# Four graph layers on one core: the row of attention scores goes to all partitions by two DMAs through a line in DRAM

## The chip, the cores and the metric

The kernel runs on one core of a Trainium2 chip. The core has a matrix engine (PE, with its weight loads shown as PEld), a vector engine (DVE), a scalar engine (ACT), a general engine (POOL, also called GpSimd) and a queue engine (SP) that issues DMAs. Each engine works through its own list of instructions in order and waits at a semaphore where the next one needs something that is not there yet. The metric is the device time of one execution in microseconds, as the median of several runs.

## The reference

The input is 128 graphs of 128 nodes with 256 features each, and one 128x128 adjacency matrix per graph. Four layers follow each other, each with a residual and a layer norm: first a gated graph network of three steps, then three graph attention layers.

```python
# layer 0: three steps of message passing with a GRU cell
for i in range(3):
    m = einsum('bnd,de->bne', h, weight[i])
    aggr = einsum('bst,bsd->btd', A, m)
    h = gru_cell(aggr, h, w_ih, w_hh, b_ih, b_hh)
x = layernorm(x + h)
# layers 1 to 3: attention
Wh = einsum('bnf,of->bno', x, W)
f_i, f_j = Wh @ a1, Wh @ a2
e = leaky_relu(f_i[:, :, None] + f_j[:, None, :], 0.2)
e = where(adj == 0, -inf_like, e)
x = layernorm(x + einsum('bij,bjo->bio', softmax(e, axis=2), Wh))
```

In the sum `f_i[:, :, None] + f_j[:, None, :]` the second term is the same row of 128 scores for every node i. That row is what this document is about: it is computed as a column (one score for each node, a node being a partition) and is needed as a row on all 128 partitions.

## The kernel before

The 128 graphs are worked on in 32 groups of G = 4. A group passes through `gru` (three steps) and then `gat` (three attention layers, `for l in range(3)`). All matrix products are in float32. The GRU products of a step are done by `strassen` (line 649, the great majority of the matmuls) into five PSUM buffers named gate; all other products and transposes use three PSUM buffers named bank. Work buffers of one size share a pool: `k2` has 27 buffers of 128x512 floats, `k4` has 18 of 128x1024, `v` has 36 of 128x4.

Nothing is issued in the order in which it is written. Every operation is handed to a `Plan` with the engines that may do it and a cost in ns for each. The plan walks through time: an operation starts when its inputs have come (the producer's end plus a latency for each pair of engines), when its engine is free, and when its buffers are; among those that are ready the more urgent goes first. It repeats the walk six times with due times taken from the walk before and keeps the shortest. Each engine's list is then written out in the order found. For a DMA the plan counts the issue on SP, then `LATENCY["SP"]` = 4000 ns, then a correction `lag`. `LATER` shifts the stages of a group against each other, so that GRU matmuls of one group stand between the attention steps of another.

In one attention layer of one group, in order: the column sums `f` (8 reductions on DVE, line 850, four for each side) and in layers 1 and 2 a scaling (line 854); the row; the sum with the mask and its maximum (line 885, DVE, four); the leaky ReLU (line 889, ACT); the exponential (line 906, ACT); a turn of the 128x128 blocks by `turned`, which splits the halves of the floats (line 404 or 406), issues a DMA transpose on SP (line 516) and joins the halves (line 510 or 406); in layers 1 and 2 a scaling (line 918); then on PE the product of attention and features (line 956), two evictions, the product with the weights (line 967), and the residual (line 973). The next layer's sums start from there.

The row itself is made, in the first 28 groups, by one PE transpose of `f` (line 862; `f` is a 128x128 buffer of its own pool with a score in every 32nd column, so that the rows of the four graphs fall on partitions 0, 32, 64 and 96), an eviction by ACT or DVE (line 866, shown as line 404 or 406 for the copy's helper), and four GpSimd partition broadcasts (line 869) into `e_`. That operation needs a GpSimd library, loaded at the start (line 997) and exchanged for the standard one after the last use. The last four groups (`LAST` = 4) make the row by four PE transposes (line 879) and read it from PSUM.

Two other places use SP: the loads of features and adjacency (lines 681, 682, 801) and the store of the result (line 982), and `thirds` (line 540), which turns the hidden state between GRU steps by three DMA transposes for the product with the adjacency matrix (line 716).

Of the kernel before, what the change touches and what calls it, by code (L numbers as in the profile page):

```python
# [10 lines left out]
F32 = mybir.dt.float32  # L11
# [5 lines left out]
P = 128  # L17
D = 256
KC = D // P
G = 4  # L20
GN = G * P
# [287 lines left out]
def adj_resnorm_kernel(  # L309
# [14 lines left out]
    nc = tc.nc  # L324
    B = x.shape[0]
    NG = B // G
    LAST = 4
# [2 lines left out]
    consts = ctx.enter_context(tc.tile_pool(name="consts", bufs=1))  # L330
    work = ctx.enter_context(tc.tile_pool(name="work", bufs=1))
    psum = ctx.enter_context(tc.tile_pool(name="psum", bufs=1, space=bass.MemoryType.PSUM))


    pools = {"gru": 4, "xs": 2, "am": 5, "k2": 27, "k4": 18, "f": 3, "mv": 4, "st": 6, "v": 36,
             "mb": 4, "gate": 5, "bank": 3}
    own = ({"k2": 7, "k4": 10, "gate": 0, "bank": 0, "v": 5, "st": 0}, {"k2": 3, "k4": 1, "bank": 0, "v": 4, "st": 0})
    floats = {"gru": 0, "k4": 1024, "xs": 1024, "f": 128, "mv": 8, "st": 6, "v": 4, "mb": GN // 2}
# [5 lines left out]
    slots = {t: [(psum if t in ("gate", "bank") else work).tile([P, w], F32, name=f"{t}{i}")  # L344
                 for i in range(n)] for t, (n, w) in tags.items() if w}

    def T(b):
        if b.at is None:
            width = 1
            for s in b.shape:  # L350
                width *= s
            at = slots[b.tag][b.slot][:, 0:width]
            if len(b.shape) == 2:
                at = at.rearrange("p (a b) -> p a b", b=b.shape[-1])
            elif len(b.shape) == 3:
                at = at.rearrange("p (a b c) -> p a b c", b=b.shape[-2], c=b.shape[-1])
            b.at = at
        return b.at

    def bank():  # L360
        return Buf("bank", GN)
# [3 lines left out]
        b.at = t  # L365
        return b

    for t in slots["f"]:
        nc.vector.memset(t, 0.0)

# [3 lines left out]
    ident = consts.tile([P, P], F32)  # L374
# [27 lines left out]
    def copy(e, dst, src):  # L402
        if e == "ACT":
            nc.scalar.copy(dst, src)  # L404
        else:
            nc.vector.tensor_copy(dst, src)  # L406
# [431 lines left out]
    def gat(g, xc, no, stage):  # L838
# [3 lines left out]
        for l in range(3):  # L842
            prio = stage(g, STEPS + l)
            if g == 0:
                score_weights(l, (prio[0], -2))
            f, fi = Buf("f", G, P // G), Buf("v", G)
            side = lambda h, f=f, fi=fi: T(f)[:, :, 0] if h else T(fi)
            for h in (1, 0):
                for b in range(G):
                    plan.op({"DVE": 345}, lambda e, b=b, h=h, l=l, side=side, xc=xc: nc.vector.scalar_tensor_tensor(  # L850
# [2 lines left out]
                if l:  # L853
                    plan.op({"DVE": 78}, lambda e, h=h, side=side, rstd=rstd: nc.vector.tensor_mul(
                        side(h), side(h), T(rstd)), reads=[((fi, f)[h], b) for b in range(G)] + [rstd],
                        writes=[((fi, f)[h], b) for b in range(G)], prio=prio, port=BOTH)
            e_, pT, y = Buf("k2", G, P), Buf("k2", G, P), Buf("k4", G, D)
            top, nmax, den, rden = Buf("v", G), Buf("v", G), Buf("v", G), Buf("v", G)
            b_ = bank()
            if g < NG - LAST:  # L860

                plan.op({"PE": 109}, lambda e, b_=b_, f=f: nc.tensor.transpose(
                    T(b_)[:, 0:P], T(f).rearrange("p b h -> p (b h)"), ident),
                    reads=[(f, b) for b in range(G)], writes=[b_], prio=prio)
                row = Buf("k2", P)
                plan.op({"ACT": 160, "DVE": 207}, lambda e, b_=b_, row=row: copy(e, T(row), T(b_)[:, 0:P]),
                        reads=[b_], writes=[row], prio=prio)
                for b in range(G):
                    plan.op({"POOL": 292}, lambda e, row=row, b=b, e_=e_: nc.gpsimd.partition_broadcast(  # L869
                        T(e_)[:, b, :], T(row)[b * P // G:b * P // G + 1, 0:P]), reads=[row], writes=[(e_, b)], prio=prio, port=BOTH, holds=False)  # L870
# [5 lines left out]
            else:  # L876
                def fn(e, b_=b_, f=f):
                    for b in range(G):
                        nc.tensor.transpose(T(b_)[:, b * P:(b + 1) * P],
                                            T(f)[:, b, 0:1].to_broadcast([P, P]), ident)  # L880
# [40 lines left out]
            else:  # L921
                b_ = bank()
# [119 lines left out]
```

## Time and profile before

| What | Value |
|---|---|
| median of 3 runs | 2499.49 us (2498.88 to 2499.88) |
| the profiled execution | 2499.94 us |
| its span, first to last instruction | 2497.9 us |
| mean granted PE clock | 0.997 |
| SP's DMA issues | 366 DMA transposes, 128 loads and stores of x, adj and out, 13 loads of weights |
| DMA queue of SP | 455952 packets, 158.65 MB, 29.9% of the 16 DMA engines' span |
| partition broadcasts (line 869) | 336, 138.4 us of POOL |
| transposes of line 862 | 84 |

The profile lists busy time for each engine, groups of instructions by line with their mean time, what each engine waited for, and for DMAs the time from the issue to the landing, that is until the semaphore has its full count. A matmul is pipelined: the time shown for one overlaps the next, so what it takes from PE is the distance from its start to the next start.

### The profile page before, as it was taken

The page shows a single profiled execution, that of the slowest core. Times are in us where ns is not written, and L with a number is a line of the kernel's source. Part 1 is how long each engine was busy: PE and PEld are TensorE (multiplying, and loading weights), DVE is VectorE, ACT ScalarE, POOL GpSimd, SP SyncE. Part 2 cuts the span into 40 slices and gives each one's busy share as a digit, 9 for nine tenths or more (in the row PEclk, how much of TensorE's full clock was granted, in tenths as well). Part 3 has the DMA queues.
Part 4 walks back from the last instruction along what each step waited for, and adds up shares of the span by engine and source line. Part 5 has one row for each costly group of instructions (what it writes and reads, how often), then busy time and mean ns, then how long its engine had stood idle before and what let it go on. Part 6 is the DMA issues. An engine that isn't in the chain of part 4 may idle for free.

```text
span 2497.9 us, 42545 instructions
## 1 busy us (share of the span) xinstructions
PE 2469.1 (99%) x13492; PEld 2180.1 (87%) x13492; DVE 2164.0 (87%) x6461; ACT 1925.7 (77%) x4835; POOL 781.9 (31%) x999
## 2 busy tenths in 40 slices
PE   8999999999999999999999999999999999999998
PEld 7888888888888888888888888888888888888877
DVE  6789888989888988889988889988889988877797
ACT  6578777888778787788887778887787888666577
POOL 2232233422334332334333334233333332211001
PEclk9999999999999999999999999999999999999999
DMA  5223233233333332333242233333233333110101
GB/s 148 56 56 64 60 76 69 64 81 60 76 64 73 72 81 60 73 68 73 68 77 68 61 80 68 73 71 74 60 77 68 76 65 68 26 39 18 38 1 35
DMA packets 456609, 161.38 MB, mean 65 GB/s; under 512 B 389184, under 2 KB 454720, under 8 KB 456384
## 3 DMA queue, kind: packets, MB, share of 16 engines
q1 hardware_dynamic: 455952, 158.65, 29.9%
q8 instruction: 106, 1.74, 0.3%
q14 instruction: 119, 0.97, 0.1%
q10 hardware_dynamic: 432, 0.01, 0.0%
HBM read 45.89 MB, written 16.78 MB: 25 GB/s over the span
## 4 chain that ended last, share of the span: by engine, by line
PE 86%; DVE 6%; ACT 4%; DMA 2%; issue 1%; POOL 0%; POOLq 0%; ACTq 0%; DVEq 0%
PE gate L649 63%; PE bank L967 10%; PE bank L956 6%; PE bank L716 3%; PE bank L719 2%; DVE nobody L850 2%; DMA k<-k 1%; DVE k L973 1%; ACT k L906 1%; ACT k L404 1%; DMA xs<-in_x_dram 1%; ACT k L510 1%; DVE k L406 1%; DVE k L654 1%; PE bank L822 0%
## 5 line engine op out<-in xcount | busy, mean ns | idle before, releaser
L649 PE MATMUL gate<-k,whs 128*128 128x256 f32 x4032 | 1205.2, 381 | 3.5 <-ACT k L742 1.6
L649 PE MATMUL gate<-k,wcs 128*128 128x256 f32 x4032 | 1199.3, 379 | 1.3 <-ACT wcs L404 1.3
L649 PEld LDWEIGHTS gate<-k,wcs 128*128 128x128 f32 x4032 | 766.0, 190 | 105.8 <-ACT wcs L404 1.8
L649 PEld LDWEIGHTS gate<-k,whs 128*128 128x128 f32 x4032 | 741.2, 190 | 107.8 <-ACT k L742 9.6
L654 DVE TENSOR_TENSOR k<-gate,k 128x512 f32<-128x512 f32 x576 | 388.4, 685 | 125.6 <-PE gate L649 80.4
L563 POOL TENSOR_TENSOR v<-v,neghalf 128x4 f32<-128x4 f32 x128 | 159.3, 1244 | 843.5 <-DVE v L601 460.9
L967 PE MATMUL bank<-gwT,k 128*128 128x256 f32 x1536 | 349.6, 380 | 1.6 <-DVE k L406 0.8
L967 PEld LDWEIGHTS bank<-gwT,k 128*128 128x128 f32 x1536 | 290.1, 190 | 43.7 <-DVE k L406 3.6
L850 DVE SCALAR_TENSOR_TENSOR nobody<-k,wa 128x256 bf16<-128x256 f32 x768 | 297.7, 427 | 0.7 <-ACT k L582 0.7
L753 ACT ACTIVATE k<-k,brz 128x256 f32<-128x256 f32 (+1 forms) x384 | 229.6, 624 | 71.1 <-DVE k L654 71.0
L618 POOL TENSOR_TENSOR k<-k,k 128x256 f32<-128x256 f32 x272 | 232.9, 867 | 104.1 <-DVE k L792 37.9
L404 ACT COPY k<-bank 128x512 f32<-128x512 f32 (+1 forms) x272 | 155.1, 572 | 112.0 <-PE bank L956 56.3
L735 ACT COPY k<-gate 128x512 f32<-128x512 f32 x288 | 167.9, 584 | 87.2 <-PE gate L649 83.7
L536 POOL TENSOR_TENSOR k<-k 128x512 f32<-128x512 f32 (+1 forms) x143 | 155.9, 1090 | 239.1 <-DVE k L792 189.4
L404 ACT COPY k<-k 128x512 bf16<-128x512 bf16 (+1 forms) x265 | 175.7, 694 | 53.8 <-DVE k L792 27.3
L869 POOL PARTITION_BROADCAST k<-k x336 | 138.4, 512 | 240.3 <-DVE k L406 149.1
L590 ACT ACTIVATE nobody<-k 128x256 bf16<-128x256 f32 x384 | 157.0, 415 | 60.5 <-DVE k L973 60.3
L510 ACT COPY k<-k 128x1024 uint16<-128x1024 uint16 x163 | 189.9, 1166 | 17.1 <-DMA k<-k 15.2
L956 PEld LDWEIGHTS bank<-k,k 128*128 128x128 f32 x1536 | 183.8, 192 | 11.0 <-DVE k L918 3.7
L956 PE MATMUL bank<-k,k 128*128 128x128 f32 x1536 | 190.2, 277 | 2.4 <-ACT k L510 1.5
L782 ACT ACTIVATE k<-k,bi 128x512 f32<-128x512 f32 x192 | 136.6, 726 | 66.4 <-DVE k L779 52.5
L973 DVE SCALAR_TENSOR_TENSOR k<-bank,v,k 128x256 f32<-128x256 f32 x384 | 166.9, 476 | 23.0 <-PE bank L967 22.8
(110 smaller groups left out, 3296.7 us busy)
## 6 DMA issues: line engine op xcount, KB each, us to landing
xs<-in_x_dram SPq DMA_DIRECT2D x32, 512.0 KB, 3.9
k<-in_x_dram SPq DMA_DIRECT2D x32, 512.0 KB, 4.1
out_dram<-k SPq DMA_DIRECT2D x32, 512.0 KB, 2.9
am<-in_adj_dram SPq DMA_DIRECT2D x32, 256.0 KB, 4.2
k<-k SPq DMA_TRANSPOSE x366, 3.1
k<-in_gnn_wT_dram SPq DMA_DIRECT2D x3, 256.0 KB, 4.7
k<-in_w_ihT_dram SPq DMA_DIRECT2D x2, 384.0 KB, 5.7
k<-in_w_hhT_dram SPq DMA_DIRECT2D x2, 384.0 KB, 6.7
```

The source lines that it names most:

```text
L404: nc.scalar.copy(dst, src)
L510: nc.scalar.copy(flat().bitcast(U16).rearrange("p (q h) -> p q h", h=2), T(rows).bitcast(U16).rearrange("p (h q) -> p q h", h=2))
L563: plan.op({"POOL": 980}, lambda e: nc.gpsimd.tensor_tensor(T(rstd), T(ve), neghalf, ALU.pow), reads=[ve], writes=[rstd], prio=prio, port=B ...
L618: nc.vector if e == "DVE" else nc.gpsimd).tensor_tensor(T(t)[:, j, :], a(), b(), ALU.subtract),
L649: nc.tensor.matmul(T(dst)[:, j * H:(j + 1) * H], T(w)[:, m, gt, :], moving(m, ms)[1](), start=first and n == 0, stop=n == len(todo) - 1, s ...
L654: plan.op({"DVE": 602}, lambda e: nc.vector.tensor_add(T(o)[:, :, j * H:(j + 1) * H], T(b_).rearrange("p (g n) -> p g n", g=2), T(part).re ...
L735: plan.op({"ACT": 475}, lambda e: nc.scalar.copy(T(dst), T(src)), reads=[src], writes=[(dst, 0), (dst, 1)], prio=prio)
L753: nc.scalar.activation(T(o)[:, gt, n0:n1], src(), AF.Tanh, bias=brz[:, gt * KC + c:gt * KC + c + 1], scale=0.5)
L850: plan.op({"DVE": 345}, lambda e, b=b, h=h, l=l, side=side, xc=xc: nc.vector.scalar_tensor_tensor(next(nobody[1]), T(xc)[:, b, :], 1.0, T( ...
L956: nc.tensor.matmul(T(b_)[:, b * P:(b + 1) * P], T(xc)[:, b, c * P:(c + 1) * P], T(pT)[:, b, :], start=True, stop=True)
L967: nc.tensor.matmul(T(b_)[:, (b - b0) * D:(b - b0 + 1) * D], T(aT[k])[:, b * P:(b + 1) * P], T(gwT)[:, l, k, :], start=(k == 0), stop=(k == ...
L973: nc.vector.scalar_tensor_tensor(T(y)[:, b, :], T(b_)[:, (b - b0) * D:(b - b0 + 1) * D], T(rden)[:, b:b + 1], T(xc)[:, b, :], op0=ALU.mult ...
```

## The change

In the first 28 groups the transpose, its eviction and the four broadcasts are replaced by two DMAs on SP. The first writes the 128x4 scores into a line of 512 floats in DRAM, in the order graph, node; the elements that follow each other in the line come from different partitions. The second reads that line once for each of the 128 partitions into `e_`. `f` becomes a 128x4 buffer of pool `v`; the pool `f` with its three memsets goes, and a pool `line` of four DRAM tiles comes. Both library loads go. The plan counts each DMA as 400 ns on SP with a lag of -1300 ns. The last four groups keep their way.

```diff
+    far = ctx.enter_context(tc.tile_pool(name="far", bufs=1, space=bass.MemoryType.DRAM))
-    pools = {"gru": 4, "xs": 2, "am": 5, "k2": 27, "k4": 18, "f": 3, "mv": 4, "st": 6, "v": 36,
+    pools = {"gru": 4, "xs": 2, "am": 5, "k2": 27, "k4": 18, "line": 4, "mv": 4, "st": 6, "v": 36,
...
-    for t in slots["f"]:
-        nc.vector.memset(t, 0.0)
...
+    ROW = -1300
...
-            f, fi = Buf("f", G, P // G), Buf("v", G)
-            side = lambda h, f=f, fi=fi: T(f)[:, :, 0] if h else T(fi)
+            f, fi = Buf("v", G), Buf("v", G)
+            side = lambda h, f=f, fi=fi: T(f) if h else T(fi)
...
-            b_ = bank()
             if g < NG - LAST:
-                plan.op({"PE": 109}, lambda e, b_=b_, f=f: nc.tensor.transpose(
-                    T(b_)[:, 0:P], T(f).rearrange("p b h -> p (b h)"), ident),
-                    reads=[(f, b) for b in range(G)], writes=[b_], prio=prio)
-                row = Buf("k2", P)
-                plan.op({"ACT": 160, "DVE": 207}, lambda e, b_=b_, row=row: copy(e, T(row), T(b_)[:, 0:P]),
-                        reads=[b_], writes=[row], prio=prio)
-                for b in range(G):
-                    plan.op({"POOL": 292}, lambda e, row=row, b=b, e_=e_: nc.gpsimd.partition_broadcast(
-                        T(e_)[:, b, :], T(row)[b * P // G:b * P // G + 1, 0:P]), reads=[row], writes=[(e_, b)], prio=prio, port=BOTH, holds=False)
-                if g == NG - LAST - 1 and l == 2:
-                    plan.op({"POOL": 7000}, lambda e: nc.gpsimd.load_library(library_config.standard),
-                            reads=[(e_, b) for b in range(G)], writes=[Buf(None)], prio=prio)
+                line = Buf("line", GN)
+                plan.op({"SP": 400}, lambda e, f=f, line=line: nc.sync.dma_start(
+                    T(line)[0].rearrange("(b q) -> q b", b=G), T(f)),
+                    reads=[(f, b) for b in range(G)], writes=[line], prio=prio, lag=ROW)
+                plan.op({"SP": 400}, lambda e, line=line, e_=e_: nc.sync.dma_start(
+                    T(e_).rearrange("p b q -> p (b q)"), T(line).to_broadcast([P, GN])),
+                    reads=[line], writes=[(e_, b) for b in range(G)], prio=prio, lag=ROW)
...
-        nc.gpsimd.load_library(library_config.all_libraries[10])
```

More of the change, by code (lines that the diff above doesn't have):

```diff
@@ L332, in adj_resnorm_kernel @@
     psum = ctx.enter_context(tc.tile_pool(name="psum", bufs=1, space=bass.MemoryType.PSUM))
-    pools = {"gru": 4, "xs": 2, "am": 5, "k2": 27, "k4": 18, "f": 3, "mv": 4, "st": 6, "v": 36,
+    far = ctx.enter_context(tc.tile_pool(name="far", bufs=1, space=bass.MemoryType.DRAM))
+    pools = {"gru": 4, "xs": 2, "am": 5, "k2": 27, "k4": 18, "line": 4, "mv": 4, "st": 6, "v": 36,
              "mb": 4, "gate": 5, "bank": 3}
     own = ({"k2": 7, "k4": 10, "gate": 0, "bank": 0, "v": 5, "st": 0}, {"k2": 3, "k4": 1, "bank": 0, "v": 4, "st": 0})
-    floats = {"gru": 0, "k4": 1024, "xs": 1024, "f": 128, "mv": 8, "st": 6, "v": 4, "mb": GN // 2}
+    floats = {"gru": 0, "k4": 1024, "xs": 1024, "mv": 8, "st": 6, "v": 4, "mb": GN // 2}
     tags = {t: (n, floats.get(t, 512)) for t, n in pools.items()}
@@ L343, in adj_resnorm_kernel @@
     plan = Plan({t: n for t, (n, _) in tags.items()}, own)
-    slots = {t: [(psum if t in ("gate", "bank") else work).tile([P, w], F32, name=f"{t}{i}")
+    spaces = {"gate": psum, "bank": psum, "line": far}
+    slots = {t: [spaces.get(t, work).tile([1 if t == "line" else P, w], F32, name=f"{t}{i}")
                  for i in range(n)] for t, (n, w) in tags.items() if w}
@@ L858, in gat @@
             top, nmax, den, rden = Buf("v", G), Buf("v", G), Buf("v", G), Buf("v", G)
-            b_ = bank()
             if g < NG - LAST:
-                plan.op({"PE": 109}, lambda e, b_=b_, f=f: nc.tensor.transpose(
-                    T(b_)[:, 0:P], T(f).rearrange("p b h -> p (b h)"), ident),
-                    reads=[(f, b) for b in range(G)], writes=[b_], prio=prio)
-                row = Buf("k2", P)
-                plan.op({"ACT": 160, "DVE": 207}, lambda e, b_=b_, row=row: copy(e, T(row), T(b_)[:, 0:P]),
-                        reads=[b_], writes=[row], prio=prio)
-                for b in range(G):
-                    plan.op({"POOL": 292}, lambda e, row=row, b=b, e_=e_: nc.gpsimd.partition_broadcast(
-                        T(e_)[:, b, :], T(row)[b * P // G:b * P // G + 1, 0:P]), reads=[row], writes=[(e_, b)], prio=prio, port=BOTH, holds=False)
-                if g == NG - LAST - 1 and l == 2:
-                    plan.op({"POOL": 7000}, lambda e: nc.gpsimd.load_library(library_config.standard),
-                            reads=[(e_, b) for b in range(G)], writes=[Buf(None)], prio=prio)
+                line = Buf("line", GN)
[5 more added lines that the diff above has]
+                    reads=[line], writes=[(e_, b) for b in range(G)], prio=prio, lag=ROW)
                 rows, keys, port = (lambda b, e_=e_: T(e_)[:, b, :]), lambda b: [], BOTH
             else:
+                b_ = bank()
                 def fn(e, b_=b_, f=f):
@@ L879, in fn @@
                         nc.tensor.transpose(T(b_)[:, b * P:(b + 1) * P],
-                                            T(f)[:, b, 0:1].to_broadcast([P, P]), ident)
+                                            T(f)[:, b:b + 1].to_broadcast([P, P]), ident)
                 plan.op({"PE": 437}, fn, reads=[(f, b) for b in range(G)], writes=[b_], prio=prio)
```

## The prediction

> **What bounds the kernel now.** First the page's busy times, then the same by stretches of the span (columns: stretch, length, then busy time and number of instructions of each engine, granted clock, DMA share, GB/s).
>
> ```profile
> PE 2469.1 (99%) x13492; PEld 2180.1 (87%) x13492; DVE 2164.0 (87%) x6461; ACT 1925.7 (77%) x4835; POOL 781.9 (31%) x999
> ```
>
> ```profile
> 0.00:100.00 100.00, 93.15 (x441) 77.39 (x442) 68.37 (x137) 60.35 (x116) 23.07 (x30) 1.00 0.40 106
> 100.00:600.00 500.00, 496.93 (x2723) 438.19 (x2722) 436.95 (x1234) 388.99 (x959) 164.57 (x209) 1.00 0.33 67
> 600.00:1100.00 500.00, 499.54 (x2771) 442.89 (x2770) 447.77 (x1353) 402.63 (x998) 180.00 (x230) 1.00 0.34 71
> ...
> 2400.00:2498.00 98.00, 81.62 (x484) 70.53 (x484) 81.87 (x432) 76.63 (x299) 13.97 (x13) 0.93 0.07 23
> ```
>
> PE never rests in the middle: it is idle 0.46 us of 500 from 600 to 1100, 3.07 us of 500 while the pipeline of groups fills, and 16.4 us of 98 at the end, when no GRU work is left to fill gaps. So the end is set by the amount of PE work and by what makes PE wait. A shorter or longer chain elsewhere counts only if PE's list, which is in order, meets it.
>
> The third view is PE's timeline around one row transpose (start, length, engine, line, operation, tiles), with the two steps that follow it on other engines; the fourth is PE's groups, each shape apart, for that line.
>
> ```profile
> 1066.82 0.59 PE L649 MATMUL gate<-k,wcs 128*128 128x256 f32 x2
> 1067.26 0.27 PE L862 MATMUL bank<-ident,f 128*128 128x128 f32 x1
> 1067.37 0.60 PE L649 MATMUL gate<-k,whs 128*128 128x256 f32 x2
> ...
> 1068.42 1.34 POOL L869 PARTITION_BROADCAST k<-k  x4 [5.97 <-DVE k L406]
> ...
> 1068.88 0.29 DVE L885 CUSTOM_DVE_ANT_0 k<-k,am 128x128 f32<-128x128 f32 x1
> ```
>
> ```profile
> L862 PE MATMUL bank<-ident,f 128*128 128x128 f32 x84 | 23.2, 276 | 0.4 <-DVE nobody L850 0.3
> ```
>
> The transpose delays the next matmul by 0.11 us (1067.26 to 1067.37), not by its 0.28 us. From its start to the first use of the row on DVE it is 1.6 us here, and 2.1 and 2.3 us for the other two layers of that period (1096.42 to 1098.47, 1128.53 to 1130.80): 2.0 us on the mean. DVE starts on the first of four broadcasts while POOL is still at the others.
>
> Last, the DMAs (tiles, issuing queue, count, size, median us from issue to landing) and who waited for landings (waiter, awaited, total us, times, longest).
>
> ```profile
> xs<-in_x_dram SPq DMA_DIRECT2D x32, 512.0 KB, 3.9
> out_dram<-k SPq DMA_DIRECT2D x32, 512.0 KB, 2.9
> k<-k SPq DMA_TRANSPOSE x366, 3.1
> k<-in_gat_w_dram SPq DMA_DIRECT2D x3, 256.0 KB, 4.5
> bi<-in_b_ih_dram ACTq DMA_DIRECT2D x1, 3.0 KB, 2.6
> ```
>
> ```profile
> ACT k L510 <- DMA k<-k: 15.2, 21, 2.1
> ...
> DVE k L406 <- DMA k<-k: 4.6, 5, 1.4
> ```
>
> Of 366 transposes 26 came too late for ACT or DVE, by 19.8 us together. PE felt little: its own waits name line 956 behind line 510 with 1.5 us and line 716 behind a landing with 0.3 us, 1.8 of 19.8 or 9%.
>
> **The change, part by part.** *Removed from PE:* 28 groups x 3 layers = 84 transposes at 0.11 us, 9.2 us, and the 0.4 us of idle time before them: -9.6 us. PE's built list has those 84 fewer and nothing else changed in number, so PE's work is 9.2 us less for certain. All else is about waits.
>
> *Removed from DVE, ACT and POOL:* 74 evictions on DVE at 0.284 us, 10 on ACT at 0.263 us, 336 broadcasts (138.4 us of POOL), three memsets, both library loads. The plan also shifts other work: by the built lists, 45 evictions of 0.684 us go from ACT to DVE, 24 half-splits from DVE (0.718) to ACT (1.05), 20 joins from ACT (1.166) to DVE (0.718), 17 scalings of line 918 (four instructions of 0.393 us each) to ACT. The sums nearly cancel: DVE about +11 us of 2164, ACT about -7 us of 1926. Both stay below PE, so I take 0; the cover is PE's own work, and without it the +11 us would be the price.
>
> *Added to SP:* 168 issues at 0.43 us (the weight loads' issue time) are 72 us. In the built list 51 of the 84 second DMAs stand right behind their own first, so SP waits there until the line has landed, some 2.2 us after a first issue of 0.43: at most 84 x 2.2 = 185 us. SP's transposes take 366 x 1.23 = 450 us of 2498, so the queue has room. Queued behind: in 46 of 84 cases the next entry is a transpose (line 516 or 540), and ACT or DVE waits for its landing, then PE. If all were ready and 2.2 us late, 101 us of lateness at 9% would be 9 us; if none was ready, 0. The other entries between are placed by what is ready when, so I take +1.
>
> *The row's way:* two landings in a row in place of 2.0 us. The trace has no scatter of 4-byte pieces to DRAM and no load that reads one line 128 times. For the first, the ends are 2.6 us (the 3 KB load `bi`) and 4.3 us (the 6 KB load `ga`, behind two others); the nearest by direction, the store of 512 KB, has 2.9. It has a 256th of that store's bytes, so I take 2.6. For the second, also 256 KB in 128 rows of 2 KB, the nearest is the load of `gat_w`, whose three landed in 3.4 to 5.0 us, the first with no sister ahead of it; the ends are 2.6 us (fastest load of `am`, 256 KB) and 4.5; I take 3.4. Sum 6.0 us (5.2 to 8.8), which is 4.0 us more than the 2.0 (3.2 to 6.8).
>
> What hides these 4.0 us is matmuls of other groups. I counted them in both built lists, between the last matmul of line 967 and the first of line 956 in the next layer of the same group, each at its start-to-start distance in the trace (0.22 us for 256 columns, 0.11 for 128). Over the first 2200 us there are 54 such gaps: mean 22.5 us before (17.9 to 25.6), 26.5 after (20.8 to 39.4). PE's list now leaves 3.9 us more. The need is 4.0, so I take 0, at the very edge. If the cover were gone, 84 x 4.0 = 336 us would be added.
>
> *The order itself:* before, the list repeats itself exactly from group to group (gaps 25.6 and 20.2); after, it never settles, and the gap between GRU steps 1 and 2 shrinks from 34 to 22 us (medians), though 18 us occurred before, in a stretch without a wait. The unsettled stretch of before, 100 to 600, has 3.07 us idle per 500 against 0.46: over the 1600 us that were regular, (3.07 - 0.46) x 3.2 = 8 us at most, nothing at least. Of its waits, line 956 behind line 510 (1.5 us) belongs to gaps shorter than any in the new list, so I take a quarter of the 8: +2. First load at the start (5.0 us wait) and last twelve layers at the end (same PE entries after the last GRU product): 0, as nothing in them changes.
>
> Sum: -9.2 - 0.4 + 1 + 2 = -6.6 us. The profiled execution took 2499.94 us, 2.0 of it outside its span of 2497.9, and lies 0.45 above the median of 2499.49. From 2499.94 it gives 2493.3, from the median 2492.9: 2493.
>
> [...]
>
> **The rivals.** *The gain is eaten by the order (same).* PE loses 9.2 us of work, but the unsettled list costs the full 8 us: 2499.5 - 9.6 + 8 + 1 = 2499. For it: the 3.07 us; against: no gap as short as the shortest before.
>
> *The row lands late (slower).* All 16 DMA engines read one 2 KB line, and DMA transposes are queued ahead. If the first takes 2.9 us and the second 4.0, as the 512 KB loads do, the row needs 4.9 us more where the list has 3.9: each is 1.0 us late. Then DVE stands at line 885, behind which the gate sums of line 654 are queued, for which PE waits, and line 956 comes late itself. 22 of the 54 gaps are under 25 us; scaled to 84 rows, 34 tight ones at 1.0 us make +34: 2499.5 - 9.6 + 34 = 2524. It decides from 0.3 us late (34 x 0.3 = 10), that is from 6.2 us for both landings. For it: my need is already at the edge. Against: 19.8 us of late transposes cost PE 1.8 us, and the first landing may be quicker than 2.6.
>
> **How the numbers follow.** Forecast, PE's work goes and the waits stay small: 0.43, own range 2488 to 2495. Eaten by the order: 0.17. Late row: 0.40, thereof some 0.12 above 2535. A change under 0.2% (5 us) can't be told from none here. So faster 0.43, same 0.17, slower 0.40. The range runs from 2487 (neither +1 nor +2, with 3 us of PE's other waits gone as three banks serve 84 fewer users) to 2535 (1.3 us late in the same 34); about 0.05 below, 0.12 above.
>
> **What would show it.** PE busy falls by 9 us and its count by 84; DVE's idle time at the reductions with the new mask line names the line's landing in under 20 us if I am right, in over 60 us if the row is late; the two DMAs' landings read 2.6 and 3.4; PE's idle time in 600 to 1600 stays under 3 us. Wrong would make it: landings above 6.2 us in sum, transposes landing at well over 3.1 behind the new waits on SP, or a last stretch with far more idle than 16.4 us.

## The result, and the profile after

The kernel with the two DMAs takes 3158.47 us (median of five runs, 3157.48 to 3159.13) where the kernel before takes 2499.49 us beside it (2498.27 to 2500.55). The ratio is 1.2637, 95% interval 1.2618 to 1.2655: slower by 26%, far outside the range, and the wrong way.

The page's first lines of the kernel after: its span, and each engine's busy time, share and number of instructions.

```profile
span 3157.2 us, 42018 instructions
...
PE 2624.7 (83%) x13408; PEld 2289.3 (73%) x13408; DVE 2171.5 (69%) x6430; ACT 1931.8 (61%) x4839; POOL 617.4 (20%) x648
```

DVE and ACT work as long as before, and PE has its 84 instructions fewer. PE's idle time grew from 28.8 us (2497.9 - 2469.1) to 532.5 us (3157.2 - 2624.7), and its busy time grew by 155.6 us although it has less to do. Together that is the 659.3 us by which the span grew. The next view, the kernel after in stretches (columns as in the same view of before), tells where, and why busy time grew.

```profile
0.00:100.00 100.00, 92.40 (x441) 76.89 (x442) 69.56 (x134) 60.79 (x117) 22.91 (x31) 1.00 0.42 106
100.00:600.00 500.00, 419.35 (x2180) 366.67 (x2179) 349.68 (x964) 306.23 (x729) 98.10 (x106) 0.92 0.30 60
600.00:1100.00 500.00, 413.19 (x2104) 359.87 (x2103) 341.96 (x1008) 311.68 (x780) 107.90 (x112) 0.91 0.33 62
...
2600.00:3157.00 557.00, 481.95 (x2490) 421.51 (x2488) 391.92 (x1320) 330.43 (x933) 74.15 (x77) 0.93 0.17 35
```

The first 100 us, before the first row is needed, are as before. From then on PE idles in every stretch for 13 to 20% of its time (86.8 us of 500 from 600 to 1100, against 0.46 before), and the granted clock is 0.90 to 0.93 instead of 1.00. The loss is spread evenly over the groups.

Now the DMAs of the kernel after (tiles, queue, count, size, median us from issue to landing), and below them the waits (waiter, awaited, total us, times, longest), DVE's and ACT's first, SP's own last.

```profile
out_dram<-k SPq DMA_DIRECT2D x32, 512.0 KB, 3.1
...
k<-line SPq DMA_DIRECT2D x84, 256.0 KB, 5.1
...
line<-v SPq DMA_DIRECT2D x84, 2.0 KB, 10.0
```

```profile
DVE k L880 <- DMA k<-line: 559.6, 76, 15.4
ACT k L884 <- DVE v L880: 518.8, 78, 16.1
PE gate L650 <- DVE k L655: 163.6, 26, 11.4
...
PE gate L650 <- ACT k L736: 129.9, 20, 14.7
PE gate L650 <- ACT k L743: 129.6, 24, 8.8
...
ACT k L511 <- DMA k<-k: 73.5, 26, 10.0
...
DVE k L406 <- DMA k<-k: 35.2, 11, 7.2
```

```profile
SPq L865 <- DMA line<-v: 724.2, 84, 13.3
```

The first DMA writes 2 KB and lands after 10.0 us (8.7 at the least, 14.3 at the most). The store of 512 KB to the same kind of memory still lands after 3.1. Two chains follow from it. DVE stands at the masked sum (line 880, 885 before) for 559.6 us, in 76 of 84 cases, and ACT behind DVE; PE then waits at line 650 for gate sums and evictions that are queued behind them (lines 655, 736, 743). SP, on the other side, stands at the second DMA in all 84 cases, 724.2 us in all, and DMA transposes behind it are issued late (lines 511 and 406: 108.7 us of waits against 19.8 before). The timeline of the kernel after around one row shows both (start, length, engine, line, operation; in brackets the idle time before it); the lines are SP's, DVE's and PE's.

```profile
1507.75 0.36 SPq L862 DMA_DIRECT2D line<-v  x1
1517.12 0.33 SPq L865 DMA_DIRECT2D k<-line  x1
1517.55 4.61 SPq L517 DMA_TRANSPOSE k<-k  x2
...
1522.30 0.29 DVE L880 CUSTOM_DVE_ANT_0 k<-k,am 128x128 f32<-128x128 f32 x1 [6.04 <-DMA k<-line]
...
1524.57 0.70 PE L650 MATMUL gate<-k,whs 128*128 128x256 f32 x2 [2.33 <-DVE k L655]
...
1530.75 1.22 PE L650 MATMUL gate<-k,whs 128*128 128x256 f32 x2 [4.18 <-ACT k L743]
```

Between the first issue (1507.75) and the second (1517.12) lie 9.4 us in which SP issues nothing, and two transposes go out right behind the second. The row is used at 1522.30, 14.6 us after the first issue, where the plan had counted twice 3.1 us.

### The profile page after: what moved, and what is told of

Read it like the earlier page. It is cut to its first block, busy times and chain, and to the rows that moved or that the text cites. A ratio compares the mean times of both kernels' runs of the same rounds, so it can differ in the third digit from the quotient of the medians.

```text
span 3157.2 us, 42018 instructions
## 1 busy us (share of the span) xinstructions
PE 2624.7 (83%) x13408; PEld 2289.3 (73%) x13408; DVE 2171.5 (69%) x6430; ACT 1931.8 (61%) x4839; POOL 617.4 (20%) x648
## 4 chain that ended last, share of the span: by engine, by line
PE 27%; DMA 20%; DVE 7%; ACT 3%; issue 2%; POOL 0%; SPq 0%; POOLq 0%; ACTq 0%; DVEq 0%
PE gate L650 18%; DMA line<-v 13%; DMA k<-line 5%; PE bank L962 4%; PE bank L951 3%; DVE nobody L851 2%; DMA k<-k 2%; PE bank L720 1%; DVE k L655 1%; DVE k L968 1%; DVE k L880 1%; ACT k L884 1%; DVE k L406 1%; PE bank L717 1%; DVE k L619 0%
## 5 line engine op out<-in xcount | busy, mean ns | idle before, releaser
L650 PE MATMUL gate<-k,whs 128*128 128x256 f32 x4032 | 1289.5, 403 | 457.1 <-DVE k L655 163.6
L650 PE MATMUL gate<-k,wcs 128*128 128x256 f32 x4032 | 1263.7, 397 | 21.8 <-DVE k L406 14.5
L650 PEld LDWEIGHTS gate<-k,whs 128*128 128x128 f32 x4032 | 791.2, 203 | 590.6 <-DVE k L655 160.0
L650 PEld LDWEIGHTS gate<-k,wcs 128*128 128x128 f32 x4032 | 810.1, 201 | 147.0 <-DVE k L406 15.3
L880 DVE CUSTOM_DVE_ANT_0 k<-k,am 128x128 f32<-128x128 f32 x336 | 80.9, 291 | 559.6 <-DMA k<-line 559.6
L884 ACT ACTIVATE k<-k,v 128x128 f32<-128x128 f32 x384 | 127.6, 392 | 536.2 <-DVE v L880 518.8
L404 ACT COPY k<-k 128x512 bf16<-128x512 bf16 (+1 forms) x297 | 216.3, 741 | 63.7 <-DVE k L793 50.1
L511 ACT COPY k<-k 128x1024 uint16<-128x1024 uint16 x143 | 165.1, 1160 | 77.2 <-DMA k<-k 73.5
L404 ACT COPY k<-bank 128x512 f32<-128x512 f32 x244 | 141.3, 585 | 104.5 <-DVE k L619 30.1
L619 POOL TENSOR_TENSOR k<-k 128x256 f32<-128x256 f32 x93 | 83.0, 893 | 599.4 <-DVE k L793 385.8
```

Source lines behind the costliest of these rows:

```text
L511: nc.scalar.copy(flat().bitcast(U16).rearrange("p (q h) -> p q h", h=2), T(rows).bitcast(U16).rearrange("p (h q) -> p q h", h=2))
L619: nc.vector if e == "DVE" else nc.gpsimd).tensor_tensor(T(t)[:, j, :], a(), b(), ALU.subtract),
L650: nc.tensor.matmul(T(dst)[:, j * H:(j + 1) * H], T(w)[:, m, gt, :], moving(m, ms)[1](), start=first and n == 0, stop=n == len(todo) - 1, s ...
L884: plan.op({"ACT": 292}, lambda e, b=b, fi=fi, e_=e_: nc.scalar.activation(T(e_)[:, b, :], T(e_)[:, b, :], AF.Prelu, bias=T(fi)[:, b:b + 1] ...
```

## The experiments

Line numbers shift by a few from kernel to kernel; the tiles' names say which row is meant. Where no interval is given, the time is that of one run. The kernel before took 2499.0 to 2499.9 us beside these kernels.

### Without the first DMA

```diff
-                plan.op({"SP": 400}, lambda e, f=f, line=line: nc.sync.dma_start(
-                    T(line)[0].rearrange("(b q) -> q b", b=G), T(f)),
+                plan.op({"SP": 400}, lambda e: None,
...
-                    T(e_).rearrange("p b q -> p (b q)"), T(line).to_broadcast([P, GN])),
+                    T(e_).rearrange("p b q -> p (b q)"), x[g * G, 0:2, :].rearrange("n d -> (n d)").unsqueeze(0).to_broadcast([P, GN])),
```

> The changed kernel in its own order, with the first DMA (84 scatters of scores into the line) left out; the second reads rows of x in place of the line, so the attention scores are not the reference's. Theory A, the first landing (10.0 us against the 3.1 that the order was made for) makes the row late and that is the loss: SP no longer waits before the second, the row comes earlier than planned or at most 1 us late, and the time falls to 2490 to 2520 us. Theory B, the second DMA (5.1 against 3.1) or the new order itself is a large part of the loss: 2600 us or more. Theory C, both share it by their lateness (6.9 and 2.0 us of 8.9): about 2500 + 84 x 2.0 = 2670 us.

It took 2488.38 us, 11 us less than before. The second DMA, 256 KB read from one 2 KB row, landed in 3.6 us (median of 84). Of this kernel, its page's busy times and the one wait for the row:

```profile
PE 2455.2 (99%) x13408; PEld 2178.2 (88%) x13408; DVE 2170.5 (87%) x6430; ACT 1916.2 (77%) x4839; POOL 621.4 (25%) x648
```

```profile
DVE k L879 <- DMA k<-in_x_dram: 2.6, 6, 0.8
```

PE's list is the same entry for entry as in the kernel after, so its order costs nothing, and neither does the second DMA. The whole loss, 3158.47 - 2488.38 = 670 us, hangs on the first DMA.

### The first DMA, with somebody waiting on one side only

Here the first DMA stays, and its landing holds up either SP or DVE. In the first kernel SP waits as in the change, but DVE reads a constant in place of the row:

```diff
-                    T(e_).rearrange("p b q -> p (b q)"), T(line).to_broadcast([P, GN])),
+                    dump, T(line)[:, 0:3 * P].to_broadcast([P, 3 * P])),
...
-                rows, keys, port = (lambda b, e_=e_: T(e_)[:, b, :]), lambda b: [], BOTH
+                rows, keys, port = (lambda b: ident), lambda b: [], BOTH
```

> The changed kernel in its own order, both DMAs as in the change, SP waiting for the first landing, but the second lands in a buffer that nobody reads and the masked sums read a constant in place of the row (so the attention scores are not the reference's). DVE never waits for the row; the transposes queued on SP behind the wait are late as in the change. Theory A: 2490 to 2560 us. Rival, the queue behind the wait is the loss: 84 x 6.9 us of it, 2850 to 3070 us.

In the second the second DMA reads from x and so needs no line, and DVE overwrites a piece of `f` ahead of the masked sum, for which the first DMA must have landed:

```diff
-                    T(e_).rearrange("p b q -> p (b q)"), T(line).to_broadcast([P, GN])),
+                    T(e_).rearrange("p b q -> p (b q)"), x[g * G, 0:2, :].rearrange("n d -> (n d)").unsqueeze(0).to_broadcast([P, GN])),
...
+                    if b == 0 and g < NG - LAST:
+                        nc.vector.memset(T(f)[:, 0:1], 0.0)
```

> The changed kernel in its own order, with the slow first DMA kept but nothing on SP waiting for it: the second DMA reads rows of x (so the attention scores are not the reference's), and DVE waits for the first landing just ahead of the masked sums, by a small write over the scores that the first DMA reads. So the row is late on DVE by 10.0 - 6.2 = 3.8 us a layer, and SP is free. Theory A, lateness on DVE goes through to PE: 2488 + 84 x 3.8 x about 0.9 = 2770 us (2700 to 2830). Rival, the loss comes from the transposes queued on SP behind the second DMA's wait: 2490 to 2560 us.

They took 2848.10 us and 2860.86 us, that is 360 and 372 us above the kernel without the first DMA, the one just under its rival's range, the other just above its theory's. The sum, 732 us, is near the 670 us of both together. It is no clean split, though: in the first kernel the second DMA moves 192 KB and not 256, and in the second more than DVE's wait for the row is late, as its rows below show. Of the kernel in which SP alone waits, SP's wait for the line, then those of DVE and ACT:

```profile
SPq L866 <- DMA line<-v: 627.4, 78, 12.2
```

```profile
DVE k L407 <- DMA k<-k: 122.7, 29, 10.1
...
DVE am L689 <- DMA am<-in_adj_dram: 109.2, 19, 13.9
ACT k L512 <- DMA k<-k: 104.6, 32, 9.0
```

What is queued behind SP's wait comes late: 227.3 us of waits for transposes where before had 19.8, and 109.2 for the adjacency loads. I had expected this side to be the small one, and by itself it costs about half.

Where DVE alone waits, SP goes on at once, and the second DMA is issued while the first is on its way. Its row by line, issues and landings:

```profile
L865 SPq DMA_DIRECT2D k<-in_x_dram x84: 347/456/4151, 164.0 to 2654.3; - x84
...
DMA to landing us min/median/max: 3.4/9.7/14.3
```

The same load of 256 KB landed in 3.6 us when no such store was ahead of it, and now takes 9.7. So behind the slow store the load on the same queue lands 6.1 us later as well. To take the wait off SP would therefore not have been enough. How the store holds up the load is not shown.

The waits of this kernel, DVE's for the first DMA and for the load, then those for transposes:

```profile
DVE v L882 <- DMA line<-v: 163.2, 56, 6.1
DVE k L883 <- DMA k<-in_x_dram: 120.3, 46, 11.5
...
ACT k L511 <- DMA k<-k: 61.7, 28, 9.2
...
DVE k L406 <- DMA k<-k: 27.2, 14, 5.9
```

Of DVE's 283.5 us only 163.2 are for the first landing itself; 120.3 are for the load that the store held up. The transposes are late too, by 88.9 us, against 29.9 without the first DMA. So the 372 us are not DVE's wait alone.

### The plan told the measured landings

```diff
-                    reads=[(f, b) for b in range(G)], writes=[line], prio=prio, lag=ROW)
+                    reads=[(f, b) for b in range(G)], writes=[line], prio=prio, lag=5600)
...
-                    reads=[line], writes=[(e_, b) for b in range(G)], prio=prio, lag=ROW)
+                    reads=[line], writes=[(e_, b) for b in range(G)], prio=prio, lag=700)
```

> The changed kernel, with the order made for the landings that were measured (10.0 us for the first, 5.1 for the second) in place of 3.1 each. Theory D, the loss comes from an order that expects the row too early, and matmuls of other groups can cover 15 us per layer: 2500 to 2600 us. Theory E, the longer chain itself binds (buffers held longer, not enough other work): over 2800 us, with PE idle for the row as before.

It took 2681.76 us, between the two theories' ranges. A plan that knows of 10.0 and 5.1 us puts other work into the gap, and DVE's wait for the row falls from 559.6 to 27.0 us. That takes back 477 us of the 670. The other 193 stay: SP still stands 221.9 us behind the first DMA, and what comes through its queue, transposes and loads, is late, as the waits of this kernel show.

```profile
ACT k L511 <- DMA k<-k: 106.9, 48, 9.3
ACT k L404 <- DMA xs<-in_x_dram: 40.2, 10, 7.5
DVE k L406 <- DMA xs<-in_x_dram: 39.1, 6, 7.7
...
DVE k L880 <- DMA k<-line: 27.0, 11, 7.1
```

### What makes the first DMA slow

The kernel before, with an added store in each layer that nobody reads, of six kinds in turn. The edit's core, of two of the kinds:

```diff
+                    if kind == 0:
+                        nc.sync.dma_start(sink[0][0].rearrange("(b q) -> q b", b=G), T(fi))
+                    elif kind == 1:
+                        nc.sync.dma_start(sink[1][0].rearrange("(b q s) -> q b s", b=G, s=16)[:, :, 0], T(fi))
```

> The kernel before, with one extra store to DRAM per layer that nobody reads, in six kinds in turn; their landings are read from the trace. Kinds: (1) 512 pieces of 4 bytes packed, as in the change; (2) the same 64 bytes apart; (3) the same 512 bytes apart; (4) 128 pieces of 4 bytes packed; (5) 128 pieces of 16 bytes packed; (6) 128 pieces of 4 bytes 64 bytes apart. Theory F, pieces that share a 64-byte stretch wait for each other: 10 us for (1) and (4), under 4 for (2), (3), (6), and about 4 for (5). Theory G, each small write costs the same wherever it goes (about 16 ns each in a row): 10 us for (1), (2), (3), 4 us for (4), (5), (6). The time stays near the kernel before, 2499 to 2530 us, as nobody waits for these stores.

For this kernel, a row for each line: the issues (ns min/median/max, first and last start), and below each its landings. L865 is the change's own pattern, 512 pieces of 4 bytes packed in DRAM; L867 the same pieces 64 bytes apart; L873 writes 128 pieces of 16 bytes, packed.

```profile
L865 SPq DMA_DIRECT2D sink<-v x14: 367/372/375, 157.9 to 2138.2; - x14
...
DMA to landing us min/median/max: 8.3/8.4/10.9
...
L867 SPq DMA_DIRECT2D sink<-v x14: 359/371/372, 194.5 to 2163.1; - x14
...
DMA to landing us min/median/max: 1.8/1.9/3.3
...
L873 SPq DMA_DIRECT2D sink<-v x14: 337/344/352, 261.9 to 2282.2; - x14
...
DMA to landing us min/median/max: 1.4/1.4/2.6
```

The same number of pieces of the same size lands in 1.9 us when they lie 64 bytes apart. Neither the number of pieces nor their size is the price by itself, then; what counts here is that 4-byte pieces out of different partitions lie next to each other in DRAM (8.4 us). Theory G is out, and the landings of theory F hold in the main but for the 16-byte pieces, which at 1.4 us land sooner than it said. The kernel took 2510.67 us.

A second set of stores, built the same way, varied distance and number. Two of its kinds:

```diff
+                    if kind == 0:
+                        nc.sync.dma_start(sink[0][0].rearrange("(q s) -> q s", s=2)[:, 0:1], T(fi)[:, 0:1])
...
+                    else:
+                        nc.sync.dma_start(sink[5][0].rearrange("(q s) -> q s", s=1)[0:16], T(fi)[0:16, 0:1])
```

> The kernel before with one extra store of scores to DRAM per layer that nobody reads, six kinds in turn, landings read from the trace: 128 pieces of 4 bytes (1) 8 bytes apart, (2) 16 bytes apart, (3) 32 bytes apart; (4) 128 pieces of 8 bytes packed; 4-byte pieces packed from (5) 64 and (6) 16 partitions. Theory H, each piece waits for the others in its 64-byte stretch: (1) and (4) about 4 us, (2) and (3) 1.4 to 2.5, (5) and (6) about 8. Rival, what counts is how many neighbours the whole run has: (5) 4 us, (6) under 2.

The kernel took 2498.41 us. Both sets together:

| Store, pieces of 4 bytes unless told | set | landing us, min / median / max |
|---|---|---|
| 512 pieces, packed | first | 8.3 / 8.4 / 10.9 |
| 128 pieces, packed | first | 7.4 / 8.1 / 8.9 |
| 64 pieces, packed | second | 6.4 / 6.9 / 8.2 |
| 16 pieces, packed | second | 1.3 / 1.3 / 3.7 |
| 128 pieces, 8 bytes apart | second | 2.9 / 3.2 / 5.1 |
| 128 pieces, 16 bytes apart | second | 1.4 / 2.2 / 3.3 |
| 128 pieces, 32 bytes apart | second | 1.4 / 1.4 / 3.1 |
| 128 pieces, 64 bytes apart | first | 1.4 / 1.4 / 3.8 |
| 512 pieces, 64 bytes apart | first | 1.8 / 1.9 / 3.3 |
| 512 pieces, 512 bytes apart | first | 1.7 / 1.8 / 3.2 |
| 128 pieces of 8 bytes, packed | second | 2.7 / 3.0 / 4.0 |
| 128 pieces of 16 bytes, packed | first | 1.4 / 1.4 / 2.6 |

From 32 bytes' distance on the price is gone (1.4 us), at 8 it is 1.8 us (3.2 against 1.4). It hardly grows from 128 packed pieces to 512 (8.1 to 8.4 us), and 16 have none (1.3 us). Neither expectation for the second set fits all of it. The wait within a stretch of 64 bytes, in theory F and in the second set's theory H, was the author's guess and is not shown: 16 packed pieces fill one such stretch, and they land in 1.3 us. The packet records of the traces narrow it: counted from each issue on, the last of the first DMA's 512 packets of 4 bytes ends after 1.2 us (median of 84), in the kernel after as in the one of the next section, whose pieces lie apart. The packed pieces are sent as fast, and the 8 us lie between that and the landing. What happens there is left open.

### The kernel after, with the pieces apart

```diff
-                    T(line)[0].rearrange("(b q) -> q b", b=G), T(f)),
+                    slots["line"][line.slot][0].rearrange("(b q s) -> q b s", b=G, s=16)[:, :, 0], T(f)),
```

> The changed kernel in its own order with both waits kept; only the pieces of the first DMA lie 64 bytes apart (16 times the line), so that it lands in about 1.9 us in place of 10.0. The second reads the first 512 floats of that longer line as they are, filled with x at the start by four loads, so the attention scores are not the reference's. Theory A (the packed pieces' landing time is the whole loss; the two waits and the new order cost nothing while the landings stay within the 6.2 us of the order): 2486 to 2500 us. Rival (a wait on SP between two DMAs costs by itself): 2520 us or more.

2492.15 us (median of six runs), ratio 0.9971 (0.996 to 0.9982): 0.3% faster than before. Order, both waits, number and size of pieces are those of the change. Of this kernel, the first DMA's line (issues as in the probe's view, then landings), and the second's:

```profile
L864 SPq DMA_DIRECT2D line<-v x84: 359/360/701, 163.1 to 2285.9; - x84
...
DMA to landing us min/median/max: 1.7/1.9/4.0
...
L867 SPq DMA_DIRECT2D k<-line x84: 332/332/571, 165.5 to 2287.7; - x84
...
DMA to landing us min/median/max: 3.0/3.2/4.8
```

SP still stands at the second DMA, 101.0 us in 65 cases, and yet the time is within 4 us of that without the first DMA. The distance between pieces alone moves the time by 666 us. That shows the cause of the loss: the late landing of packed pieces.

### Versions that compute everything

Pieces of 16 bytes (the four scores of a node side by side) need no transposed store, but then the row comes with its graphs interleaved, and somebody has to read it in steps of 16 bytes. Four ways were tried: the steps stay through all of the layer; DVE's masked sum undoes them (once with one throw-away buffer, for results that nobody reads, for each engine, once with DVE's two); GpSimd undoes them in a copy. The common edit, and the copy's:

```diff
-                    T(line)[0].rearrange("(b q) -> q b", b=G), T(f)),
+                    T(line)[0].rearrange("(q b) -> q b", b=G), T(f)),
...
+                plan.op({"POOL": 1235}, lambda e, rw=rw, e_=e_: nc.gpsimd.tensor_copy(
+                    T(e_), T(rw).rearrange("p q b -> p b q")), reads=[rw], writes=[(e_, b) for b in range(G)], prio=prio, port=BOTH)
```

> The changed kernel in its own order; the line holds the scores node by node, so the first DMA writes 128 pieces of 16 bytes in place of 512 of 4, and the masked scores are kept node by node as well (strided views on DVE and ACT). Theory A, many small pieces make the landing: 2.6 to 4.5 us in place of 10.0, the time 2490 to 2650 us. Rival, the way through DRAM itself takes 10 us whatever the pieces: landing 9 to 10 us and 3100 to 3200 us.

> The change with 16-byte pieces in a node-by-node line, the row in a buffer of its own that the masked sums read with a stride and write packed, so that ACT works on packed scores again (one such buffer; the two throw-away buffers of each engine become one to make room). Landings 1.7 + 3.8 = 5.5 us, under the 6.2 of the order. Theory A (only landings later than planned cost): 2486 to 2500 us, under the kernel before. Rival, the strided scores on DVE cost as they did on ACT, or the one buffer makes rows wait: 2510 to 2620 us.

> As the run with 16-byte pieces and a row buffer of its own, but DVE has its two throw-away buffers again and only ACT has one. If the single throw-away buffer on DVE held that run up (its sums of line 851 took 341 us in place of 309): 2500 to 2515 us; what stays over 2488 is the strided reading on DVE (0.40 in place of 0.31 us, 336 times, 30 us of DVE). Rival, the one row buffer makes the rows wait: 2530 us again.

> As before this one, with the node-by-node row put in order by one copy on GpSimd (about 1.1 us, 84 times), so that DVE and ACT work on packed data, and with the order told the landings 2.2 and 4.2 us. Theory A: DVE and ACT have no more work than in the kernel before, PE 9.2 us less: 2486 to 2500 us. Rival, the longer chain (1.7 + 3.8 + 1.1 us against 6.2) or the copy's port sharing with DVE costs more than the 11 us gained: 2505 to 2540 us.

| Version | median us | ratio (95% interval) | landings us |
|---|---|---|---|
| steps all through the layer | 2613.82 | 1.045 (1.0433 to 1.0468) | 1.7, 3.8 |
| DVE reads in steps, one throw-away buffer each | 2534.32 | 1.0139 (1.0122 to 1.0156) | 1.7, 3.8 |
| DVE reads in steps, DVE has two | 2509.71 | 1.0041 (1.0028 to 1.0055) | 1.7, 3.8 |
| GpSimd copies, plan told 2.2 and 4.2 | 2508.04 | 1.0036 (1.0023 to 1.005) | 1.4, 3.7 |
| DVE turns blocks of 32x32 (below) | 2521.53 | 1.0092 (1.0075 to 1.0109) | 1.4, 4.8 |

The slow first landing is cured in each. In the first three the row is read in steps, which has a price; how much of their time it makes up was not tried apart. Three groups of the first version (line, engine, operation, tiles, count, busy us and mean ns, idle before and its releaser):

```profile
L886 ACT ACTIVATE k<-k,v 128x128 f32<-128x128 f32 x384 | 171.4, 514 | 40.2 <-DVE v L882 39.0 <-DVE v L855 0.5
...
L404 ACT COPY k<-k 128x1024 uint16<-128x1024 uint16 x87 | 141.4, 1625 | 29.6 <-DVE k L793 28.9 <-ACT k L754 0.2 <-issue 0.2
L882 DVE CUSTOM_DVE_ANT_0 k<-k,am 128x128 f32<-128x128 f32 x336 | 119.8, 419 | 17.7 <-DMA k<-line 17.5
```

The same groups take 392, 1040 and 291 ns in the kernel after. The 384 of the leaky ReLU include 48 of the last four groups, which are not in steps; from 200 to 2100 us, where all are, one takes 532 ns, so that ACT pays 140 ns a block. The split of halves pays 585 ns, the masked sum on DVE 128 ns (104 against the 315 ns of the kernel before). The copy on GpSimd, 84 times some 1.2 us in an engine with time to spare, adds to the row's way instead: 1.4 + 3.7 + 1.2 = 6.3 us. But its plan had allowed for more, and DVE waited for the copies only 4.5 us, so why this version is 9 us slower than before is open. The slowing of DVE beside GpSimd that its rival names (port sharing) is in the trace of the kernel before, though not what is shared: the masked sum takes 282 ns on the mean where GpSimd is idle (119 of them) and 344 ns where more than half of it runs beside a broadcast (138). In the kernel with the copies it takes 314 ns on the mean, against 310 with the pieces apart.

In the last version DVE's transpose of 32x32 blocks puts the scores of 32 nodes side by side in a partition, so that no reader needs small steps:

```diff
+                plan.op({"DVE": 80}, lambda e, f=f, ft=ft: nc.vector.transpose(T(ft), T(f)),
+                        reads=[(f, b) for b in range(G)], writes=[ft], prio=prio, port=BOTH)
+                plan.op({"SP": 400}, lambda e, ft=ft, line=line: nc.sync.dma_start(
+                    T(line)[0].rearrange("(p j) -> p j", j=32), T(ft)),
+                    reads=[ft], writes=[line], prio=prio, lag=-2200)
```

> The whole computation, with two DMAs as in the change, but no 4-byte piece: the four scores of a node stand in a 128x32 buffer, DVE turns its 32x32 blocks (one instruction more in each layer), so that each score lies beside those of the next nodes in one partition, the first DMA writes 128 pieces of 128 bytes to a line of 16 KB, the second reads four pieces of 512 bytes for each partition, and DVE's masked sum reads the row in runs of 32 floats. Theory H (the packed 4-byte store was the whole loss, and order, SP's waiting and the second DMA cost nothing, as without the first DMA and with pieces 64 bytes apart): first landing 1.4 to 1.9 us, second 3.4 to 4.2, DVE's masked sum stays near 311 ns, time 2490 to 2498, faster than before by up to 0.4%. Rival I (either the added DVE step in the chain of the row, or the 512-byte reads landing later, takes the room of some 4 us that the order has): first and second landing together with the turn above 6.2 us, time 2503 or more.

2521.53 us, in the rival's range. The turn takes 0.209 us and the first landing 1.4, but the second, now 512 pieces of 512 bytes, lands in 4.8 us. That is 6.4 us in all; the plan had been told 2.2 for the first and 3.9 for the second. DVE's wait at the masked sum in this kernel:

```profile
DVE k L887 <- DMA k<-line: 64.4, 52, 4.3
```

No version that computes everything beat the kernel before. The two that leave something out, at 2488.38 and 2492.15 us, show that 7 to 11 us are there for a row that lands in 3.6 to 5.1 us. That last version with the plan told 4.8 us wasn't tried, so that its second landing makes up the 22 us is argued, not shown.

## Why the prediction was wrong, point by point

**What failed: the first landing, taken as 2.6 us.** The step went by size ("it has a 256th of that store's bytes, so I take 2.6", ends 2.6 and 4.3). It measured 10.0, more than twice the upper end. No row of the trace had a store of pieces that lie side by side out of different partitions, and bounds taken from rows of other shapes bound nothing here. Had the upper end been open, the range would have been too. In the sum the step stood behind a 0: a need of 4.0 us against 3.9 us of further cover.

**The second landing, 3.4 us.** Right as a term: 3.6 from x, 3.2 with the pieces apart. In the kernel after it read 5.1; why it is slower there was not tried apart. Both together made 15.1 us instead of 6.0, and 8.9 us more than the 6.2 us from which the late row was to decide. 84 x 8.9 = 748 us if all of it came through; 670 did, 90%. That these lie so near is in part luck, as 169.5 us of the loss are PE's longer busy time (below) and not waiting.

**SP's blocking, +1.** Mis-sized, by the wait and by what comes through. SP stood 724.2 us instead of at most 185. Where it alone waited, 627.4 us of standing cost 360 us, 57%, where 9% had been put in. The 9% came from 26 transposes that were late by 0.8 us each on the mean (19.8 / 26), few of which PE felt. A queue that stands for 8.6 us at a time (724.2 / 84) also makes loads late (109.2 us of DVE's waits for `am` where SP alone waited, 1.7 before), and the small share of before says nothing about it.

**The late row as a rival.** Its mechanism was the right one, with its place: DVE at the masked sum, the gate sums behind it, PE at line 650. Its price, 34 tight gaps at 1.0 us, rested on a first landing of 2.9, not 10.0. DVE waited in 76 of 84 cases, not 34, 7.4 us each (559.6 / 76).

**What held.** PE's work: without the first DMA PE's idle time is 31.3 us (2486.5 - 2455.2) against 28.8 before, and its busy time 13.9 us less, so the 9.6 us are there, and some more, which was not traced. The order, +2 (0 to 8): no cost shows, as the same order ran at 2488.38. The work that moves between engines: the DVE terms that have a price add up to +6.9 us and not to the +11 put down; DVE's busy time grew by 7.5, and nothing hung on it. The sum of 2493 is near what the change gives with pieces apart, 2492.15, where the landings sum to 5.1 us. The edge of 6.2 us was not tested: the ways with 6.3 and 6.4 us are slower than before by 9 and 22 us, but their plans were told other landings.

**What wasn't in the sum at all: PE's clock.** After its gaps of more than 4 us PE gets slower, too: the clock is 0.50 to 0.59 in the 3.4 us behind them in the kernel after. Each row is one kernel with the same number of matmuls; the growth is against the kernel without the first DMA.

| Kernel | PE idle us | granted clock | PE busy us, and growth |
|---|---|---|---|
| without the first DMA | 31.3 | 0.997 | 2455.2 |
| plan told | 167.0 | 0.975 | 2513.0, +57.8 |
| SP waits alone | 289.6 | 0.951 | 2556.7, +101.5 |
| DVE waits alone | 291.2 | 0.954 | 2567.9, +112.7 |
| after | 532.5 | 0.914 | 2624.7, +169.5 |
| steps all through the layer | 110.6 | 0.995 | 2502.3, +47.1 |

In the four with the packed store each us of idle time goes with 0.34 to 0.43 us of longer matmuls (169.5 / 501.2 and 112.7 / 259.9 of growth over growth). The prediction priced a wait as its own length. The last row shows that idle time alone doesn't lower the clock as far: there PE is idle for 110.6 us but waits never longer than 3.0 us after its first load, and the clock stays at 0.995. A clock lower by 0.002 makes some 5 us of its 47.1 (0.002 x 2455.2, an estimate); what the rest is was not traced, and part of the growth in the other rows may be of that kind. The kernel after in stretches of 3.4 us (columns as before) has both kinds of gap of the timeline above, 2.33 us at 1524.57 and 4.18 us at 1530.75:

```profile
1523.80:1527.20 3.40, 1.99 (x8) 1.44 (x8) 2.50 (x6) 3.37 (x7) 3.21 (x4) 1.00 0.34 64
1527.20:1530.60 3.40, 0.00 (x0) 0.00 (x0) 0.48 (x2) 3.40 (x13) 0.40 (x1) 1.00 0.27 52
1530.60:1534.00 3.40, 3.25 (x8) 2.63 (x9) 3.40 (x13) 3.40 (x9) 1.01 (x1) 0.51 0.98 183
1534.00:1537.40 3.40, 3.40 (x35) 3.03 (x34) 3.40 (x12) 3.40 (x8) 0.00 (x0) 0.99 0.46 156
```

After the short gap the clock is 1.00, after the long one 0.51 for one stretch. Over the whole of this kernel from 100 us on, the 3.4 us after each of PE's 65 gaps of more than 4 us (up to 14.7) have a clock of 0.50 to 0.59, those after the ten gaps of 2 to 4 us anything from 0.50 to 1.00, and those after the five of 1 to 2 us 1.00. That goes with the mean of 0.914 here, and with 0.995 where no later gap is longer than 3.0 us. What sets the clock was not shown.

**The list of what would show it.** PE's count fell by 84, as said. DVE's wait at the row read 559.6 us, where over 60 was to mean a late row; the landings in sum 15.1, where above 6.2 was to be wrong; PE's idle time from 600 to 1100 alone 86.8, where under 3 was to be right for twice that stretch. So the list named the failure by its place, and the page tells it at first sight.

## What to carry to other kernels

Price a DMA by the pattern that it writes and not by its bytes: ask how long its contiguous pieces are, and whether short pieces of different partitions meet in one spot of DRAM (8.4 us packed here, 1.9 us with the same pieces 64 bytes apart); where no row of the trace shows that pattern, its cost has no upper end, and one store that nobody reads, put into the kernel before, measures it in one run. A DMA that waits for another on a queue in order costs that queue the wait (SP stood for 724.2 us here), so count what stands behind it. And where the bound engine starts to idle for microseconds at a time, look at its granted clock (0.914 here, 0.997 before) before you price the idle time at its length.

## What the runs showed of the hardware

- 4-byte pieces packed in DRAM, one from each of 64 partitions or more: 6.9 to 10.0 us to land, against 1.4 to 2.2 with 16 bytes or more between their starts and 1.4 for packed pieces of 16 bytes. Sixteen such pieces land in 1.3.
- A load of 256 KB behind such a store on the queue lands in 9.7 us instead of 3.6.
- One row of 2 KB read by all 128 partitions (256 KB) lands in 3.2 to 3.6 us where no slow store is on its way. The plain load of the same size, `am`, lands in 2.8 in the same two kernels, so a price of the shared source isn't ruled out. As four pieces of 512 bytes for each partition it takes 4.8.
- float32 in steps of 16 bytes costs ACT 532 ns for a 128x128 block instead of 392, and DVE's masked sum 419 ns in place and 401 ns from another buffer instead of 291 (kernel after) to 315 (before).
- PE's granted clock in the kernel after is 0.51 in the 3.4 us after a gap of 4.18 us and 1.00 after one of 2.33; it is 0.50 to 0.59 after each of the 65 gaps of more than 4 us.
